# A two-layer attention kernel: attn1's row sums moved behind all of attn3's values, and four units in place of two between the last squares of layer 0 and their variance

## The chip, the cores and the metric

The kernel runs on one core of one Trainium2 chip. The metric is the device time of one launch in microseconds (us). A core has a matmul engine (TensorE; PE in the profile, PEld for its weight loads), VectorE (DVE), ScalarE (ACT), GpSimd (POOL) and SyncE (SP), which here only issues DMAs. Each engine works through its own queue in order; semaphores tie the queues together.

## What is computed

The input x is (2, 512, 64, 32): two batches, 512 channels, 2048 positions (tokens). All is float32. Cut to what matters here:

```python
# layer 0: softmax attention of 8 heads of 64, with position embeddings in q and k
o = softmax(q @ k.T / 8) @ v
x = o @ Wout + bout + x
# layer 1: Nystrom attention with 256 landmarks, then a linear feed-forward map
h = layernorm(x);  q, k, v = split(h @ Wqkv);  q = q / 8
qL, kL = mean over groups of 8 tokens of q, k                 # 256 landmarks
attn1 = softmax(q @ kL.T); attn2 = softmax(qL @ kL.T); attn3 = softmax(qL @ k.T)
out = attn1 @ (pinv(attn2) @ (attn3 @ v)) + depthwise_conv33(v)   # pinv: 6 iterations
x = x + out @ Wout + bout
x = x + layernorm(x) @ w_lora.T @ W.T
```

## The kernel before

**Tiles.** Channels lie on the 128 partitions, and heads are worked in pairs of two (2 x 64 = 128 rows). There are 2 batches x 4 pairs = 8 pairs. Tokens are cut into NTB = 4 blocks of TB = 512 or NST = 16 of 128. PSUM holds matmul results in banks of 128 x 512; helpers hand them out in rotation by tag: `bank` (two buffers up to the end of layer 0, four later), `product_bank` (two), `side_bank` (one each).

**Order.** PE, DVE, ACT and POOL keep the order in which the program text issues their instructions. Python generators yield after a small piece of work (a unit), and `advance(gens, n)` lets them make up to n units and returns how many it made; an exhausted generator is dropped from the list. So the order on every engine is fixed when the program is built. SP's DMAs are ordered by the scheduler.

**End of layer 0.** Layer 0 ends, for batch 1, with a loop over the four blocks t. For each, `out0` makes the output projection (four units), and `norm0_steps`, through `statistics` (L983), the layer norm in steps: channel sums on DVE (L986, L987), the mean as a matmul (L990), subtraction (L991, DVE), squares on ACT (L994, L997) and their adding on DVE (L1002, L1003), the variance as a matmul with a constant 1/C (L1006), square root on ACT (L1008, with a table load), then a reciprocal (L1023), two multiplications by it on POOL (L1025) and DVE (L1026), and a store of the normalised block (L1027, POOL's queue). Between these steps PE is given units of two lists: `more_out`, the output projection of the next block (empty for the last one), and `more`, layer 1's work for batch 0, from `others`. That yields key and query projections (L1245, four matmuls of 512 columns each, copied by ACT at L1248, reduced by DVE at L1250 and L1253) and, in their midst, for the pair before, `attend` (L1274: landmark scores, exponentials, and on DVE row sums, reciprocal and normalisation of X, L1297 to L1303, head by head) and `gram` for each head (L1305: matmuls of the normalised X at L1313 into two banks, 257 and 129 columns wide, copied by ACT at L1320; DVE's L1322 takes column sums from the copies).

**The loop over pairs in layer 1.** For each pair n in the order batch 1, then batch 0, `pinv` (L1531) runs five iterations for both heads. In each, `square` transposes one block (`flip`: PE at L1528, ACT's copy at L1529) and multiplies (L1538, tiles pa and pb), and DVE combines (L1551, `less`). After each iteration it calls `chunk(c)` (L1955), which does other pairs' work, so that PE is busy while DVE finishes:

- the pair before (`before`, while c < `n_ones`; n_ones is 4 for n up to 5, else 3): attn1 for token block c: scores (L1595), exponentials (L1600), an add of the two landmark halves on DVE (`attn1_add`, L1604), the product with the pinv's result (`attn1_values`, L1611, tile av), row sums (`attn1_sums`: `sums_of`, L779, four matmuls against a tile of ones, 32 columns of the array each; ACT's copy at L1619) and `attn1_inverse`: reciprocal on DVE (L1624), then eight DMAs on SP that spread it over the rows (`spread`, L790). In the next chunk `attn1_end` multiplies av by it on DVE (L1631) and adds it to the convolution's result on POOL (L1632).
- the pair behind (`after`, absent for the last pair): attn3 for key blocks 2c and 2c+1: scores (L1367), exponentials (L1376), adds on DVE (L1381), and `attn3_values` (L1388, eight records of 256 columns, 64 columns of the array each).

In `chunk` the units stand in this order: attn1 scores and add, attn3 scores and adds, attn1 values, attn3 values of 2c, attn1 sums, attn3 values of 2c+1, attn1 inverse. The next thing on PE is the flip of the next iteration.

Of the kernel before, what the change touches and what calls it, by code (L numbers as in the profile page):

```python
# [663 lines left out]
def fast_path(  # L664
# [89 lines left out]
    def block_of(pool, tag, name):  # L754
        return pool.tile([P, KC, TB], F32, tag=tag, name=name)
# [37 lines left out]
    def advance(gens, n=1):  # L793


        made, i = 0, 0
        while made < n and i < len(gens):
            got = next(gens[i], gens)
            if got is gens:
                gens.pop(i)  # L800
            elif got is GAP:
                i += 1
            else:
                made += 1
        return made

    def drain(gen):
        for _ in gen:
            pass
# [49 lines left out]
    class Heads0:  # L859
# [61 lines left out]
        def values(self):  # L921
            for t in range(NTB):
                values_of_tokens(self.v, t, self.xbs[t], lambda k: wv_sb[:, k, self.cols], self.name)
                yield
# [289 lines left out]
    class Pair:  # L1214
# [310 lines left out]
        def flip(self, X, name):  # L1525
# [3 lines left out]
            nc.scalar.copy(X[:, 1, :P], tp[:, :P])  # L1529

        def pinv(self, chunk, last):  # L1531


# [27 lines left out]
            for it in range(PINV_ITERS - 1):  # L1561
                for h in range(2):
                    pr = square(M[h], f"pa_{it}_{h}_{self.name}")
                    less_in_blocks(R[h], 3.5 * CUBE, M[h], pr)
                    less_in_blocks(M[h], 3.25 / rest, M[h], pr)
                for h in range(2):
                    pr = square(R[h], f"pb_{it}_{h}_{self.name}")
                    less_in_blocks(M[h], rest, M[h], pr)
                chunk(it)
# [134 lines left out]
    def finish1_units(b, os, early):  # L1704
        for t in range(NTB):
            if t == NTB - 1 and early:
                f = early.pop()
                yield from f.out_units()
                yield from f.norm_units()
                yield from f.map_units(lambda m, name: bank(name))  # L1710
                return
            xb = block_of(lpool, "xr", f"xb_g_{b}_{t}")
            f = Finish1(b, t, os, xb, lambda: block_of(lpool, "xn", f"xn_g_{b}_{t}"), True)
            yield from gap(3 if t else 2)
            yield from f.out_units()
            yield from f.norm_units()
            yield from f.map_units(lambda m, name: bank(name))
# [59 lines left out]
    def others(b, xhs, last, after=lambda t: None):  # L1777

        for hp in range(1, NPAIR):
            pair = pairs[b][hp]  # L1780
            pair.begin()
            units = pair.keys_and_queries(kvpool, "k", xhs, after if hp + 1 == NPAIR else lambda t: None)
            next(units)
            yield
            yield from beside(last.front(), units)
            yield from units
            last = pair
# [8 lines left out]
    more = [others(0, xhs, pairs[0][0], load_next)]  # L1796
    b = B - 1

    def as_block(tile):
        return tile.rearrange("p a b -> p (a b)").rearrange("p (k n) -> p k n", k=KC)  # L1800
# [7 lines left out]
    def norm0(t):  # L1808
        part = apool.tile([P, 2, TB], F32, tag="acc", name=f"part_f0_{t}")
        return norm0_steps(b, t, xbs_[t % 2], xns_[t % 2], part)  # L1810

    def out0(t):
        xb = xbs_[t % 2]
        nc.sync.dma_start(xb, chunked(x[b])[:, :, t * TB : (t + 1) * TB])
        return out0_units(b, t, xb, oTs)
# [4 lines left out]
    for t in range(NTB):  # L1820
        more_out = [out0(t + 1)] if t + 1 < NTB else []
        advance(more)

        next(norm)
        advance(more_out or more)
        if last is not None:
            next(last)
        advance(more_out or more)
        next(norm)
        advance(more_out, 2)  # L1830
        advance(more, 2)

        next(norm)
        last = norm
        while more_out:
            advance(more_out)
        if t + 1 < NTB:
            norm = norm0(t + 1)
            next(norm)
# [50 lines left out]
    def late_buffer(name):  # L1890

        return block_of(xpool, "xb", name).rearrange("p k n -> p (k n)")
# [37 lines left out]
    for n, pair in enumerate(todo):  # L1930
        before = todo[n - 1] if n else None
        after = todo[n + 1] if n + 1 < len(todo) else None
        if n + 2 < len(todo):
            todo[n + 2].prefetch_w()
        if n == NPAIR + 2:
            before.load_o(kvpool.tile([P, S], F32, tag="k", name=f"o2_{n - 1}"))
        if n == NPAIR + 3:

            xb = as_block(kvpool.tile([P, NST, P], F32, tag="v", name="xb_g_early"))
            xn = lambda: block_of(lpool, "xn", "xn_g_early")  # L1940
            early.append(Finish1(1, NTB - 1, [p.o for p in todo[:NPAIR]], xb, xn, True))
            before.load_o(late_buffer(f"o2_{n - 1}"))
        pair.iteration_start()
        while vals:
            advance(vals)
        if after:
            after.prefetch()
            after.attn3_begin()
        if n + 2 < len(todo):
            vals = [values(n + 2)]  # L1950
        if n:
            q = late_buffer if n > NPAIR + 1 else lambda name: kvpool.tile([P, S], F32, tag="k", name=name)
            pair.prefetch1(q(f"q2_{pair.name}"))

        def chunk(c):  # L1955
            nonlocal landmarks
            if before and 0 < c <= n_ones:
                before.attn1_end(c - 1)
            if n == NPAIR and c == 1:

                finish.append(finish1_units(1, [p.o for p in todo[:NPAIR]], early))
            advance(finish)
            if c == NTB:
                if after:
                    landmarks = after.landmarks_values()
                    next(landmarks)
                    drain(convolution(n + 1))
                else:
                    advance(finish, 2)
                return  # L1970
            ones_before = before if c < n_ones else None
            if ones_before:
                if c:
                    before.attn1_scores(c, 0)
                    before.attn1_scores(c, 1)
                before.attn1_add(c)
            if after:
                for s, bank_of in ((2 * c, product_bank), (2 * c + 1, bank)):
                    after.attn3_scores(s, bank_of)
                    after.attn3_add(s)  # L1980
            else:
                advance(finish)
            if ones_before:
                before.attn1_values(c)
            if after:
                after.attn3_values(2 * c)
            else:
                advance(finish)
            if ones_before:
                before.attn1_sums(c)  # L1990
            if after:
                after.attn3_values(2 * c + 1)
            if ones_before:
                before.attn1_inverse(c)
            if n == NPAIR + 2 and c % 2:
                advance(finish)

        def last(i):
            nonlocal start
            if i == 1 and after:  # L2000
                next(landmarks)
                drain(landmarks)
                start = after.start_values()
            if i == 2 and after:
                next(start)
            else:
                advance(vals)
            if i == 3 and after:
                next(start)
            if n_ones < NTB:  # L2010

                if i == 0:
                    before.attn1_scores(n_ones, 0)
                    before.attn1_scores(n_ones, 1)
                    before.attn1_add(n_ones)
                if i == 1:
                    before.attn1_values(n_ones)
                if i == 2:
                    before.attn1_sums(n_ones)
                if i == 3:  # L2020
                    before.attn1_inverse(n_ones)
                if i == 5:
                    before.attn1_end(n_ones)
            if i == 5:
                pair.attn1_scores(0, 0)
                pair.attn1_scores(0, 1)
            advance(finish)

        landmarks = start = None
        n_ones = NTB if n + 2 < len(todo) else NTB - 1  # L2030
        pair.pinv(chunk, last)

    def last_attn1():
# [156 lines left out]
```

## Time and profile before

| what | us |
|---|---|
| median of three runs (lowest, highest) | 2738.82 (2737.63, 2741.3) |
| the profiled execution's own time | 2739.02 |
| its span, first to last instruction | 2737.2 |
| PE busy in it | 2695.4 (98%) |
| DVE, ACT, POOL busy | 1631.7, 906.3, 162.0 |
| PE idle ahead of L1006 (variance), longest | 3.7 |
| PE idle ahead of L779 in attn1 (row sums, 128 matmuls) | 0.0 |

In the lines that follow, a timeline line has the start in us, the time it covers, the engine, the line of the kernel, the instruction, output<-inputs, the array's shape in use for matmuls (contraction rows\*columns), shapes, and how many were merged; in brackets the idle time ahead of it and what ended it. A float32 matmul appears as two records. A line of stretches has the length, then for PE, PEld, DVE, ACT and POOL the busy time (and instructions), then the granted clock of PE, the share of the DMA engines and GB/s. A busy PE in the profile is not PE at its peak: the ends of matmuls are modelled, so short stops between matmuls hide in busy time and are read from the starts.

### The profile page before, as it was taken

To read this page: it belongs to the slowest core of one execution; us is meant where nothing else is said; L and a number is where in the kernel's file an instruction comes from. 1 tells how busy PE (TensorE), PEld (TensorE's weight loads), DVE (VectorE), ACT (ScalarE), POOL (GpSimd) and SP (SyncE) were. 2 spreads that over 40 slices of the span, in tenths; PEclk is the share of its full clock that TensorE was granted. 3 is DMA by queue.
4 is the path that set the end of the run, shared out by engine and by line. 5 is a ranking of instruction groups with operands and counts; after the bars stand their busy time and mean duration, and the time that the engine had idled before them with its cause. 6 is when DMAs were issued, how large, how long until landed. Compare 5 with 4: busy or idle time off the path is not lost.

```text
span 2737.2 us, 41174 instructions
## 1 busy us (share of the span) xinstructions
PE 2695.4 (98%) x16994; PEld 1361.0 (50%) x16994; DVE 1631.7 (60%) x2087; ACT 906.3 (33%) x1352; POOL 162.0 (6%) x109
## 2 busy tenths in 40 slices
PE   9999999999999999999999999999999999999999
PEld 5343343434443334344344455777677666655344
DVE  3867777664557765656667544445544645465565
ACT  1434444434334334444422223223323223231210
POOL 0101011000001100000002000000000000000000
PEclk9999999999999999999999999999999999999999
DMA  4100000212111200012024632312211112111211
GB/s 147 41 11 24 24 24 24 86 36 70 32 63 57 97 24 20 24 40 77 24 89 163 209 120 93 103 34 87 81 37 62 59 44 87 44 60 53 89 39 47
DMA packets 111476, 173.99 MB, mean 64 GB/s; under 512 B 16176, under 2 KB 67888, under 8 KB 106672
## 3 DMA queue, kind: packets, MB, share of 16 engines
q1 hardware_dynamic: 105136, 150.00, 16.9%
q0 software_dynamic: 5440, 20.97, 2.1%
q8 instruction: 135, 2.21, 0.3%
q14 instruction: 61, 0.50, 0.1%
q10 hardware_dynamic: 704, 0.31, 0.0%
HBM read 90.87 MB, written 63.57 MB: 56 GB/s over the span
## 4 chain that ended last, share of the span: by engine, by line
PE 91%; DVE 5%; DMA 1%; ACT 1%; SPq 1%; issue 1%; POOL 0%; DVEq 0%; ACTq 0%; POOLq 0%
PE sc_f L1072 15%; PE av_f L1102 15%; PE pp L1245 8%; PE pa L1538 5%; PE pb L1538 5%; PE vp_f L953 4%; PE vp L953 4%; PE pp_k_f L905 4%; PE yp_g L968 4%; PE yp_f L968 4%; PE fp_g L1694 4%; PE pp_q_f L905 3%; PE av L1388 2%; PE sc L1367 2%; PE sc L1595 2%; PE av L1611 2%
## 5 line engine op out<-in xcount | busy, mean ns | idle before, releaser
L1090 DVE TENSOR_TENSOR acc_f<-acc_f,p_f 128x1024 f32<-128x1024 f32 x448 | 581.3, 1297 | 209.9 <-ACT p_f L1080 181.4
L1080 ACT ACTIVATE p_f<-sc_f 128x1024 f32<-128x1024 f32 x512 | 496.7, 1022 | 563.9 <-PE sc_f L1072 561.2
L1072 PE MATMUL sc_f<-q_f,k_f 64*64 64x512 f32 x4096 | 491.1, 594 | 2.7 <-ACT p_f L1080 2.7
L1102 PE MATMUL av_f<-p_f,v_f 64*64 64x512 f32 x4096 | 484.3, 589 | 0.0
L1102 PEld LDWEIGHTS av_f<-p_f,v_f 64*64 64x64 f32 x4096 | 156.5, 133 | 283.0 <-issue 283.0
L1072 PEld LDWEIGHTS sc_f<-q_f,k_f 64*64 64x64 f32 x4096 | 145.8, 133 | 285.6 <-issue 261.9
L1245 PE MATMUL pp<-xh,w 128*128 128x512 f32 x512 | 229.5, 600 | 0.7 <-ACT q L1248 0.7
L1538 PE MATMUL pa<-M 128*128 128x192 f32 (+1 forms) x640 | 153.1, 384 | 6.0 <-ACT M L1529 6.0
L1245 PEld LDWEIGHTS pp<-xh,w 128*128 128x128 f32 x512 | 95.3, 191 | 121.3 <-issue 113.8
L1538 PE MATMUL pb<-R 128*128 128x192 f32 (+1 forms) x640 | 149.3, 380 | 0.0
L1538 PEld LDWEIGHTS pa<-M 128*128 128x128 f32 x640 | 109.3, 195 | 27.6 <-ACT M L1529 9.1
L953 PEld LDWEIGHTS vp_f<-wv_f,x 128*128 128x128 f32 x1024 | 115.7, 192 | 13.5 <-issue 11.8
L953 PE MATMUL vp<-w,xh 128*128 128x128 f32 x1024 | 120.9, 276 | 0.0
L953 PEld LDWEIGHTS vp<-w,xh 128*128 128x128 f32 x1024 | 117.0, 192 | 7.2 <-issue 4.6
L905 PE MATMUL pp_k_f<-x,wk_f 128*128 128x512 f32 x256 | 116.0, 606 | 2.8 <-DVE k_f L908 2.4
L953 PE MATMUL vp_f<-wv_f,x 128*128 128x128 f32 x1024 | 118.7, 277 | 0.0
L1538 PEld LDWEIGHTS pb<-R 128*128 128x128 f32 x640 | 106.5, 190 | 23.2 <-DVE M L1551 0.4
L905 PE MATMUL pp_q_f<-x,wq_f 128*128 128x512 f32 x256 | 114.2, 598 | 0.8 <-DVE q_f L908 0.5
L968 PE MATMUL yp_g<-o,wo_f 128*128 128x512 f32 x256 | 114.8, 597 | 0.0
L968 PE MATMUL yp_f<-q_f,wo_f 128*128 128x512 f32 x256 | 113.5, 598 | 0.8 <-DVE xr_f L975 0.8
L1120 POOL TENSOR_TENSOR q_f<-q_f,rinv_f 128x512 f32<-128x512 f32 x32 | 46.7, 1459 | 1039.3 <-DMA rinv_f<-acc_f 761.1
L1551 DVE SCALAR_TENSOR_TENSOR R<-M,pa 128x320 f32<-128x320 f32 (+1 forms) x160 | 59.9, 416 | 67.8 <-PE pa L1538 67.8
(210 smaller groups left out, 2764.8 us busy)
## 6 DMA issues: line engine op xcount, KB each, us to landing
xh<-xh_fd SPq DMA_DIRECT2D x12, 1024.0 KB, 5.5
rinv_f<-acc_f SPq DMA_DIRECT2D x256, 32.0 KB, 1.9
xr_f<-in_x_dram SPq DMA_DIRECT2D x8, 1024.0 KB, 5.2
x_fd<-xr_f POOLq DMA_DIRECT2D x8, 1024.0 KB, 4.8
xh_fd<-xn_f POOLq DMA_DIRECT2D x8, 1024.0 KB, 4.7
k_fd<-k SPq DMA_DIRECT2D x32, 256.0 KB, 2.9
q_fd<-q SPq DMA_DIRECT2D x32, 256.0 KB, 2.9
k<-k_fd SPq DMA_DIRECT2D x8, 1024.0 KB, 6.6
```

Source lines behind the costliest of these rows:

```text
L905: nc.tensor.matmul(pp, lhsT=w_sb[kind][:, k, cols], rhs=xbs[t][:, k, :], start=k == 0, stop=k == KC - 1)
L953: nc.tensor.matmul(vp[:, j * P : (j + 1) * P], lhsT=xb[:, k, j * P : (j + 1) * P], rhs=w_of(k), start=k == 0, stop=k == KC - 1,)
L968: nc.tensor.matmul(yp, lhsT=wo_sb[:, k, m * P : (m + 1) * P], rhs=oTs[k][:, toks], start=k == 0, stop=k == NPAIR - 1,)
L1072: nc.tensor.matmul(sc[r * D : (r + 1) * D, h, :], lhsT=hd.k[rows, lo : lo + D], rhs=hd.q[rows, t * TB : (t + 1) * TB], start=True, stop=True,)
L1080: nc.scalar.activation(p, sc, AF.Exp, scale=D**-0.5)
L1090: nc.vector.tensor_tensor(acc, first if c == 1 else acc, p, ALU.add)
L1102: nc.tensor.matmul(av[r][half, :], lhsT=hd.v[keys, c, half], rhs=pp[keys, h, :], start=c == 0, stop=c == NST - 1,)
L1245: nc.tensor.matmul(pp, lhsT=self.w[j][:, c, :], rhs=xhs[t][:, c, :], start=c == 0, stop=c == KC - 1)
L1367: nc.tensor.matmul(scs[h][:, j * LM : (j + 1) * LM], lhsT=self.k[rows, c * P : (c + 1) * P], rhs=self.L[0][rows, :], start=True, stop=True,)
L1538: nc.tensor.matmul(dst, lhsT=lhsT[:, k, t * P : (t + 1) * P], rhs=rhs[:, k, :], start=k == 0, stop=k == 1)
L1551: nc.vector.scalar_tensor_tensor(out, m, scale, pr, ALU.mult, ALU.subtract)
L1694: nc.tensor.matmul(fp[:, cols], lhsT=mT[:, k, m * P : (m + 1) * P], rhs=self.xn[:, k, cols], start=k == 0, stop=k == KC - 1,)
```

## The change

Two edits, both to the order of issue. The first: where the loop at the end of layer 0 made up to two units of `more_out` and then two of `more`, it now makes four of `more` if `more_out` made none. `more_out` is empty only in the last pass. The second: in `chunk`, `attn1_sums` is issued behind the second `attn3_values` rather than between the two.

```diff
@@ the loop over t at the end of layer 0
         advance(more_out or more)
         next(norm)
-        advance(more_out, 2)
-        advance(more, 2)
+        advance(more, 2 if advance(more_out, 2) else 4)
 
         next(norm)
         last = norm
@@ chunk(c)
                 after.attn3_values(2 * c)
             else:
                 advance(finish)
-            if ones_before:
-                before.attn1_sums(c)
             if after:
                 after.attn3_values(2 * c + 1)
             if ones_before:
+                before.attn1_sums(c)
                 before.attn1_inverse(c)
```

The order of PE's instructions moves so, in the last pass of the first loop: before, query projection, variance, key projection, gram of head 0, gram of head 1; after, query projection, key projection, gram of head 0, variance, gram of head 1. On DVE the two copies L1322 pass the reciprocal L1023 and the multiplication L1026; on ACT the key's copy and the two copies of head 0's gram pass the table load and the square root.

## The prediction

> **What bounds the kernel now.** I read the page first, then the list of PE's waits, then the timelines around the two edits, then granted clock by stretch. On the page:
>
> ```profile
> PE 2695.4 (98%) x16994; PEld 1361.0 (50%) x16994; DVE 1631.7 (60%) x2087; ACT 906.3 (33%) x1352; POOL 162.0 (6%) x109
> PE 91%; DVE 5%; DMA 1%; ACT 1%; SPq 1%; issue 1%; POOL 0%; DVEq 0%; ACTq 0%; POOLq 0%
> ```
>
> PE is the bound and the chain runs along it, so an edit pays only what it takes out of PE's own stream: an idle gap, or time lost between matmuls. Neither edit removes a matmul. PE's waits (total us, times, longest):
>
> ```profile
> PE pa L1538 <- ACT M L1529: 6.0, 2, 4.6
> PE var_n L1006 <- issue: 3.7, 1, 3.7
> ```
>
> The second is the variance matmul of layer 0's last block, where the projection edit acts. In the stretch 1830 to 2440 us, where the sums edit acts, PE's five listed waits come to 5.0 us and none is at L779 or L1388. So the sums wait for nothing, and that edit can only gain between the matmuls.
>
> First place, PE, then the DVE work that it waits for:
>
> ```profile
> 1492.30 1.02 PE L1245 MATMUL pp<-xh,w 128*128 128x512 f32 x2
> 1497.00 1.48 PE L1006 MATMUL var_n<-xr_f,mean_w 128*128 128x512 f32 x2 [3.68 <-issue]
> 1498.28 4.95 PE L1245 MATMUL pp<-xh,w 128*128 128x512 f32 x8
> 1503.07 3.08 PE L1313 MATMUL pr<-X 128*128 128x257 f32 x16
> 1506.16 1.13 PE L1245 MATMUL pp<-xh,w 128*128 128x512 f32 x2
> ```
>
> ```profile
> 1492.20 1.58 DVE L1269 TENSOR_TENSOR bound<-most 128x1 f32<-128x1 f32 x1
> 1496.21 0.69 DVE L1003 TENSOR_TENSOR xr_f<-xr_f 128x512 f32<-128x512 f32 x1
> 1497.75 0.69 DVE L1299 TENSOR_TENSOR X<-X,rs 128x512 f32<-128x512 f32 x1
> 1499.99 0.69 DVE L1299 TENSOR_TENSOR X<-X,rs 128x512 f32<-128x512 f32 x1
> ```
>
> "Issue" names no releaser, but L1003, which makes the variance's input, ends at 1496.90 and PE starts 0.10 later: the wait is for DVE. The next two lines matter as much: the normalised X of each head, which gram (L1313) multiplies, is ready at 1498.44 and 1500.68. The projection behind the gap took 4.95 for what takes 3.43 elsewhere (eight records 0.429 apart). The stretches say why (PE busy, then granted clock):
>
> ```profile
> 1494.17:1497.58 3.41, 0.58 (x2) 0.37 (x3) 3.34 (x8) 0.00 (x0) 0.69 (x1) 1.00 0.76 282
> 1497.58:1500.99 3.41, 3.41 (x6) 1.35 (x5) 3.24 (x7) 1.97 (x2) 0.00 (x0) 0.50 0.50 181
> 2436.24:2439.65 3.41, 1.90 (x9) 0.56 (x8) 2.83 (x4) 0.78 (x3) 0.00 (x0) 1.00 0.53 154
> 2439.65:2443.07 3.42, 2.87 (x25) 1.70 (x26) 0.69 (x3) 0.84 (x3) 0.00 (x0) 1.00 0.00 0
> 2521.57:2524.98 3.41, 1.40 (x8) 0.89 (x6) 2.66 (x3) 0.00 (x0) 1.27 (x1) 1.00 0.04 10
> ```
>
> A 3.41 us stretch that is 83% idle is followed by half clock; one 59% idle (the last line) is too, in the records of granted clock; one 44% idle is not.
>
> Second place, one chunk of today's order, and one of the last pair, which already has the order that the change makes (sums straight ahead of the flip, L1528):
>
> ```profile
> 1838.06 1.03 PE L1388 MATMUL av<-p,v 128*64 128x256 f32 x8
> 1839.02 0.64 PE L779 MATMUL rs<-acc,ones 128*32 128x256 f32 x8
> 1839.59 1.08 PE L1388 MATMUL av<-p,v 128*64 128x256 f32 x8
> 1840.60 0.33 PE L1528 MATMUL p_pa<-ident,M 128*128 128x128 f32 x1
> ```
>
> ```profile
> 2474.57 0.64 PE L779 MATMUL rs<-acc,ones 128*32 128x256 f32 x8
> 2475.14 0.33 PE L1528 MATMUL p_pa<-ident,M 128*128 128x128 f32 x1
> ```
>
> Note the array forms: 128\*64, 128\*32, 128\*64, 128\*128.
>
> [...] within a form these records start 0.216 apart, over each of the three changes 0.31. [...] the 128x1 L1269 lasts 1.58 and ends with POOL's L1025 (1490.45 to 1493.77), its seven fellows average about 0.15. [...] the trace has 1.28 ahead of the square root.
>
> **Part 1, the projections.** The condition differs only in the last pass: earlier, two output units are made and two units follow as before. In the last, four units follow. By the PE order of both kernels these are attend, a query projection, and new ahead of the variance a key projection (4 matmuls) and gram of head 0; so "four projections" is one projection and one gram more. DVE's order is the same through both L1299. So:
> - The key projection starts at 1493.15 (last record 1492.72 plus 0.43) and issues 3.43: to 1496.6. Its bank is free (the copy ended at 1489.3).
> - Gram 0 needs X at 1498.44, plus 0.10: 1498.54. PE still waits, about 1.8 between records.
> - Gram 0 issues 4 x 0.216 and 4 x about 0.13. The ordinary banks are two in rotation, so the variance takes the one that the 257-wide copy (L1320) frees: last record 1499.24, copy 0.41 later, 0.38 long, variance at 1500.08.
> - Variance: two records, with a slow first step about 0.93. Gram 1 (X at 1500.68, no wait) begins at 1501.0; its first half issues to 1501.9.
> - Its second half takes the variance's bank. ACT must end first: table load at 1501.24, 1.28, square root 0.69: 1503.2. A new wait of 1.2.
> - Second half 0.5 and start-up 0.1: next projection at 1503.9, against 1506.16 now. **Gain 2.3.**
>
> The half clock goes (of the present loss about 1.7), since the new gaps, 1.8 and 1.2, fill at most about 37% of a window on today's phase. Were a window to hold all of the first gap it would be 53% idle, between 44 and 59, unknown: half clock then costs 1.7. Bounds of this part: +0.6 and +3.5 (no bank wait); I take 2.3. Moved besides: on ACT the copies of gram 0 pass the table load (its end was worked in); on DVE two csum copies pass the 3.34 reciprocal, which may start at about 1504.3 against 1505.08; on SP the second X store passes behind k_fd and two A stores, 0.3 to 0.6 each, read only many us later. POOL's multiply and the xh store come no later than now. Work after 1506 waits on PE, not on an absolute time, so the gain is kept.
>
> **Part 2, the sums.** In the stretch 1830 to 2440 the copy L1619 occurs 23 times: five pairs with four chunks, one with three. That is where the edit moves anything; the last pair has no values to pass.
> - Now: 1838.06 to 1840.60 is 2.54.
> - After: first values group 4 x 0.216 = 0.86, the second to the sums 0.96 (as from 1838.06 to 1839.02), sums to flip 0.57 (2474.57 to 2475.14): 2.39.
> - Difference 0.15, one change of form and the slow first step after it. 23 x 0.15 = **3.5**.
>
> Does anything make PE wait? The second values start 0.67 earlier and need ACT's exponentials, which end 1.74 before that start in a first chunk, 1.09 in most, 0.80 in the worst. The copy L1619 now comes 0.86 later, just ahead of the flip's copy L1529, and the reciprocal (1.75 on DVE) 1.0 later as PE's work stands: L1551's first subtraction waits about 0.1. In the last pair that order stands already: reciprocal 2475.69 to 2477.44, subtraction at 2477.36, and flip to the first pb matmul 3.84, the same as now in the others. So zero on PE. Behind the reciprocal SP's eight spread DMAs start later, and DVE's L1631 of the next chunk, which waits for them: today 1848.94, just as they land, so 0.9 later by PE's work; POOL's multiply then locks L1604 out for about 0.5. DVE is idle 1.73 ahead of L1604, and PE's next av1 matmul is 2.1 behind L1631's end: covered. Without that cover it costs up to 0.5 a chunk. Bounds: 0.15 lost to 0.2 gained a chunk, -3.5 to +4.6; I take 3.5, for the last pair shows it.
>
> **Sum.** 2.3 + 3.5 = 5.8, from the profiled 2739.02 (span 2737.20 and 1.8 around it) to 2733.3. The median of the runs, 2738.82, is 0.2 lower: 2733.1, or -0.21%. A measurement tells about 0.2%, 5.5 us, from no change; the forecast lies at its edge.
>
> **Rivals.**
> - *The wait only moves (0.20).* Gram 0's wait for X and the square root's bank are joined by a half-clock window: part 1 gives 0.6, 2734.7. For it: the 53% above[...]. Against: 44% idle left the clock whole.
> - *The change of form isn't saved (0.10).* [...] part 2 gives 0: 2736.5. Against: the last pair's 0.57.
> - *The late sums stall the pinv step (0.06).* Sums' copy, flip's copy and reciprocal come in series at the chunk's end; if PE's pa matmul waits the copy's 0.37 in each of 23 chunks, 8.5 lost against 5.8 and 2741.5, slower. It decides from 0.25 a chunk. Against: L1529 ends 0.4 before its weight load at 1841.69 and is delayed by 0.1 or less; for it: PE did wait for this copy elsewhere.
> - *No bank wait (0.04).* 2731.9.
>
> Forecast 0.60. Its own spread with the measurement, about 0.8, puts 0.6 of it beyond -0.2%. With the last rival, and a little of the first: faster 0.43, same 0.51, slower 0.06. The range, 2731.5 to 2736.0, takes in the first rival and the upper bound and leaves out most of the second and all of the third.
>
> **What would show it.** Right: L1006's last start near 1500 with a gap near 1.8 ahead of L1313 and one near 1.2 inside it, full clock there; the projection after at 1503.9; 1838.06 to flip 2.39 in all 23 chunks; no new PE wait at L1538. Wrong: half clock again near 1500; L1529 or L1551 as PE's releaser from 1830 to 2440; a step from sums to flip over 0.57.

## The result and the profile after

| | before | after |
|---|---|---|
| median of 13 runs (lowest, highest), us | 2738.54 (2734.91, 2741.74) | 2732.43 (2731.32, 2735.85) |
| profiled execution's own time | 2739.02 | 2732.18 |
| its span | 2737.2 | 2730.4 |

The ratio of the times is 0.998, with a 95% interval of 0.9973 to 0.9988. The medians differ by 6.1 us where 5.8 were forecast.

First the page of after, busy time and the chain that ended last:

```profile
PE 2688.2 (98%) x16994; PEld 1361.7 (50%) x16994; DVE 1628.1 (60%) x2087; ACT 903.7 (33%) x1352; POOL 161.8 (6%) x109
...
PE 90%; DVE 5%; DMA 1%; SPq 1%; ACT 1%; issue 1%; POOL 0%; DVEq 0%; ACTq 0%; POOLq 0%
```

Nothing has changed in kind: the same 16994 matmul records on PE, and PE is the bound. The list of PE's waits (total us, times, longest) has lost the variance's 3.7 and has three new lines where the two edits act. Two of them:

```profile
PE pr L1313 <- DVE X L1299: 1.8, 1, 1.8
...
PE pr L1313 <- ACT rstd_n L1008: 1.2, 1, 1.2
```

The third, 0.5 ahead of the pb matmul (L1538), is shown below. To see where time was gained, I took the start of every PE record in both profiled executions and subtracted. The shift, after minus before, changes in a few places only:

| stretch (us of before) | change of the shift | what lies there |
|---|---|---|
| 0 to 1490 | -2.45 | nearly all between 11 and 37: the first loads, and a window of half clock in before, none in after; not the edit |
| 1490 to 1515 | -2.31 | the last variance of layer 0: part 1 |
| 1836 to 2411 | -3.47 | the 23 chunks: part 2 |
| 2411 to 2430 | +0.46 | the last of these chunks |
| 2430 to 2470 | -0.31 | also in the projections alone, -0.35 |
| 2470 to 2526 | +0.27 | also in the projections alone, +0.27 |
| 2526 to 2600 | +0.8 | DMAs of a spread that land about 0.9 late |

So the 6.8 us between these two spans aren't all the edit's. The first line is layer 0's first block waiting for x, and it differs from execution to execution: at 1490 the nine other profiled executions are 0.7 to 3.0 us ahead of this one of before. Near 34 us before has one window of half clock, as have two of the other nine (the projections alone and the sums alone, the two that are only 0.7 ahead); after has none. Of the kernels below only the sums alone have the last line too (0.65).

Part 1, PE in after:

```profile
1488.12 6.17 PE L1245 MATMUL pp<-xh,w 128*128 128x512 f32 x14
1496.14 1.55 PE L1313 MATMUL pr<-X 128*128 128x257 f32 x8 [1.85 <-DVE X L1299]
1497.71 1.12 PE L1006 MATMUL var_n<-xr_f,mean_w 128*128 128x512 f32 x2
1498.68 1.03 PE L1313 MATMUL pr<-X 128*128 128x257 f32 x4
1500.94 0.71 PE L1313 MATMUL pr<-X 128*128 128x129 f32 x4 [1.24 <-ACT rstd_n L1008]
1501.49 5.74 PE L1245 MATMUL pp<-xh,w 128*128 128x512 f32 x13
```

The 3.68 ahead of L1006 has become two waits, 1.85 for the X of head 0 and 1.24 for the bank that the square root must empty first. The projection behind starts at 1501.49; with the 2.45 of the start put back that is 1503.94. ACT shows the second wait from the other side:

```profile
1498.91 1.28 ACT L1008 ACT_TABLE_LOAD   x1 [0.91 <-PE var_n L1006]
1500.20 0.69 ACT L1008 ACTIVATE rstd_n<-var_n,eps 128x512 f32<-128x512 f32 x1
1500.79 0.37 ACT L1320 COPY A<-pr 128x257 f32<-128x257 f32 x1
```

The square root ends at 1500.89 and PE goes on 0.05 later. In the stretches (length, then PE busy; granted clock is the first bare number behind the engines) there is no half clock:

```profile
1493.36:1496.77 3.41, 1.56 (x6) 0.71 (x5) 3.27 (x9) 0.59 (x1) 0.00 (x0) 1.00 0.81 304
1496.77:1500.18 3.41, 2.92 (x13) 1.73 (x11) 3.31 (x7) 1.91 (x3) 0.00 (x0) 1.00 0.73 249
```

The whole first gap fell into one window, 54% idle, and the window after it was granted full clock.

Part 2, one chunk of after on PE:

```profile
1833.30 1.90 PE L1388 MATMUL av<-p,v 128*64 128x256 f32 x16
1835.12 0.64 PE L779 MATMUL rs<-acc,ones 128*32 128x256 f32 x8
1835.69 0.33 PE L1528 MATMUL p_pa<-ident,M 128*128 128x128 f32 x1
```

From 1833.30 to 1835.69 is 2.39, in place of 2.54. The same stretch is 0.15 shorter than in before in each of the 23 chunks.

### The profile page after: what moved, and what is told of

It reads as the page before. It is cut to its first block, busy times and chain, and to the rows that moved or that the text cites. A ratio compares the mean times of both kernels' runs of the same rounds, so it can differ in the third digit from the quotient of the medians.

```text
span 2730.4 us, 41173 instructions
## 1 busy us (share of the span) xinstructions
PE 2688.2 (98%) x16994; PEld 1361.7 (50%) x16994; DVE 1628.1 (60%) x2087; ACT 903.7 (33%) x1352; POOL 161.8 (6%) x109
## 4 chain that ended last, share of the span: by engine, by line
PE 90%; DVE 5%; DMA 1%; SPq 1%; ACT 1%; issue 1%; POOL 0%; DVEq 0%; ACTq 0%; POOLq 0%
PE sc_f L1072 15%; PE av_f L1102 15%; PE pp L1245 8%; PE pb L1538 5%; PE pa L1538 5%; PE vp_f L953 4%; PE vp L953 4%; PE pp_k_f L905 4%; PE yp_g L968 4%; PE yp_f L968 4%; PE fp_g L1694 3%; PE pp_q_f L905 3%; PE sc L1367 2%; PE sc L1595 2%; PE av L1611 2%; PE av L1388 2%
## 5 line engine op out<-in xcount | busy, mean ns | idle before, releaser
L1538 PE MATMUL pa<-M 128*128 128x192 f32 (+1 forms) x640 | 153.2, 385 | 6.3 <-ACT M L1529 6.3
L1538 PE MATMUL pb<-R 128*128 128x192 f32 (+1 forms) x640 | 149.3, 380 | 0.5 <-DVE M L1551 0.5
L1538 PEld LDWEIGHTS pa<-M 128*128 128x128 f32 x640 | 109.3, 195 | 27.8 <-ACT M L1529 9.4
L1538 PEld LDWEIGHTS pb<-R 128*128 128x128 f32 x640 | 106.5, 190 | 23.6 <-DVE M L1551 0.8
L1694 PE MATMUL fp_g<-xn_g,mT 128*128 128x512 f32 (+1 forms) x232 | 99.8, 580 | 0.0
```

The lines of the kernel that those rows point to most:

```text
L1538: nc.tensor.matmul(dst, lhsT=lhsT[:, k, t * P : (t + 1) * P], rhs=rhs[:, k, :], start=k == 0, stop=k == 1)
L1694: nc.tensor.matmul(fp[:, cols], lhsT=mT[:, k, m * P : (m + 1) * P], rhs=self.xn[:, k, cols], start=k == 0, stop=k == KC - 1,)
```

## The experiments

The theory: part 1 moves the wait and shortens it, with the half clock behind it gone; part 2 saves one change of array form in each chunk and makes nobody wait. The rivals: only the half clock counts in part 1; the place of the sums counts in part 2, not the number of changes. Shifts are counted as in the table above, against the profiled execution of before.

**Each part alone.** Two kernels, each with one hunk of the change.

> The projection edit alone. Theory (part 1 is a wait of its own, worth 2.3): 2736.3 against 2738.5 of before, ratio 0.9992; the projection behind gram 1 starts 2.3 earlier than before once the start-up's offset is taken out, no half clock near 1500, and the shift does not change between 1506 and 2400. Rival (the two parts are not independent, or the half clock comes back): gain under 1.

> The sums edit alone. Theory (one change of array form saved per chunk, 0.15 x 23): 2735.1, ratio 0.9987; the stretch from the first values group to the flip falls from 2.54 to 2.39 in each of 23 chunks, and one place, the pair with three chunks, gives back about 0.5 because DVE's L1631 lands late. Rival (the gain came from part 1 alone, or from the start-up's offset): ratio 1.000 and 2.54 unchanged.

The projections alone: 2736.18 against 2738.11, ratio 0.9992 (0.9986 to 0.9999). The shift changes by -2.31 at 1490 to 1515 and not at all from 1515 to 2411. The sums alone: 2734.22, ratio 0.9986 (0.9979 to 0.9992); -3.47 from 1836 to 2411. The parts add up: the two shifts in the profile are those of the whole change, to 0.01. In this execution of the second kernel the old gap stood, and cost more than in before:

```profile
1495.08:1498.49 3.41, 2.16 (x3) 1.16 (x4) 3.27 (x9) 0.03 (x1) 0.00 (x0) 0.50 0.82 309
1498.49:1501.90 3.41, 3.41 (x5) 1.34 (x5) 3.31 (x7) 1.94 (x2) 0.00 (x0) 0.50 0.42 144
```

Here 6.8 us of half clock go with the same 3.7 us gap that was followed by 3.4 in before, and the variance itself falls into it. The shift grows by 1.08 up to 1515 for that.

**The sums elsewhere.** If the number of changes of array form counts, sums ahead of both groups of values save nothing, since there the order is 64, 32, 64, 128 columns again. The edit is shown against the change; the first loop of this kernel is before's.

```diff
             if ones_before:
                 before.attn1_values(c)
+                if after:
+                    before.attn1_sums(c)
             if after:
                 after.attn3_values(2 * c)
 ...
             if ones_before:
-                before.attn1_sums(c)
+                if not after:
+                    before.attn1_sums(c)
                 before.attn1_inverse(c)
```

> As the change, but the sums stand ahead of both values groups, right behind attn1's values. Theory (only the number of changes of array form counts): as many changes as in before, so the chunk takes 2.54 again, part 2 gives nothing, 2736.3, ratio 0.9992. Rival (what counts is that the two values groups are together, or that the sums are late): 2.39, ratio 0.998. Rival 2 (sums wait for their operand when they come early): over 2.54 and slower than before.

The number in this expectation is wrong: it counts part 1, which this kernel doesn't have, and what the theory gives for it is before's own time, a ratio of 1.000. Measured: 2737.47, ratio 0.9997 (0.9989 to 1.0005), and the shift from 1836 to 2411 changes by 0.00. PE in this kernel:

```profile
1833.42 1.94 PE L1611 MATMUL av<-p,u 128*64 128x512 f32 x8
1835.29 0.64 PE L779 MATMUL rs<-acc,ones 128*32 128x256 f32 x8
1835.86 1.95 PE L1388 MATMUL av<-p,v 128*64 128x256 f32 x16
1837.73 0.33 PE L1528 MATMUL p_pa<-ident,M 128*128 128x128 f32 x1
```

From L1611, itself 64 columns wide, the forms go 64, 32, 64, 128: three changes, as in before; in the change it is two (64, 32, 128). The order is another, the changes are the same, and so is the time. What counts is the changes of form in the order, not where the sums stand.

**What is the half clock worth?** Before's order, with the gap filled: four matmuls of 512 columns that nothing reads stand ahead of the last variance, so that PE is busy in the gap and the wait itself is not shortened.

```diff
         advance(more, 2)
+        if t + 1 == NTB:
+            fill = scores_bank("fill")
+            for i in range(4):
+                nc.tensor.matmul(fill[:, i % 2, :], lhsT=mean_w, rhs=xhs[1][:, i, :], start=True, stop=True)
```

> Before's order, with four matmuls of 512 columns added ahead of the last block's variance, into a bank that nothing reads; the outputs are the reference's. They fill the 3.7 gap and remove no wait of DVE. Theory (the gap costs 3.7 by itself and about 1.7 more by the half clock behind it): no half clock near 1500, the variance starts where it did, the next query projection starts about 1.7 earlier than in before; 2736.6, ratio 0.9994. Rival (only the idle time counts): no shift, ratio 1.000.

```profile
1490.19 3.70 PE L1836 MATMUL fill<-xh,mean_w 128*128 128x512 f32 x8
1494.00 1.12 PE L1006 MATMUL var_n<-xr_f,mean_w 128*128 128x512 f32 x2
1494.96 3.60 PE L1245 MATMUL pp<-xh,w 128*128 128x512 f32 x8
```

```profile
1493.30:1496.70 3.40, 3.29 (x9) 1.27 (x8) 3.30 (x8) 1.48 (x2) 0.00 (x0) 1.00 0.68 255
1496.70:1500.10 3.40, 3.40 (x14) 2.04 (x13) 3.30 (x7) 1.57 (x4) 0.00 (x0) 1.00 0.47 160
```

The granted clock is 1.00 in both stretches. The projection takes 3.60 over eight records in place of 4.95, and the shift at 1490 to 1515 changes by -1.71, as expected. So useless work in a gap is worth 1.7 us here, and of part 1's 2.31, 0.6 is the shorter wait. Timed, this kernel gains more: 2734.48 against 2738.67, ratio 0.9986 (0.998 to 0.9993), at least 1.9 us by the interval. The gap of before can cost two windows of half clock, as in the sums-only kernel, but that hardly fills the difference: the granted clocks listed with the runs average 0.9974 for before and 0.9981 here, from which I estimate that the clock cost about 2 us less over the whole kernel ((1 - clock) x time). What the rest of the timed gain is stays open.

**Three units instead of four.** With gram 0 left behind the variance, the variance needn't wait for X.

```diff
-        advance(more, 2 if advance(more_out, 2) else 4)
+        advance(more, 2 if advance(more_out, 2) else 3)
```

> Three units in the last pass instead of four, so that gram of head 0 stays behind the variance. Theory (gram's wait for the normalised X and for the square root's bank are what is left of the gap): the variance starts at about 1497.0 in the clock of before with a gap of 0.3, gram 0 waits 0.5 for X, its second half 0.5 for the bank, the next query projection starts at 1502.3 against 1503.9 with four: 1.6 faster than the change, 2730.8, ratio 0.9972. Rival (four units are the right cover): equal to the change or slower, 2732.4.

```profile
1494.71 1.10 PE L1006 MATMUL var_n<-xr_f,mean_w 128*128 128x512 f32 x2 [0.26 <-issue]
1496.30 1.11 PE L1313 MATMUL pr<-X 128*128 128x257 f32 x4 [0.49 <-DVE X L1299]
1497.92 2.17 PE L1313 MATMUL pr<-X 128*128 128x129 f32 x12 [0.52 <-ACT rstd_n L1008]
1500.11 7.13 PE L1245 MATMUL pp<-xh,w 128*128 128x512 f32 x16
```

The three gaps come to 1.27, where the change has 3.09. The shift at 1490 to 1515 is -3.75, so 1.44 better than the change. The times, 2731.87 and 0.9977 (0.997 to 0.9984), can't tell it from the change: the profile shows it, the timing doesn't.

**A bank of its own for the variance.** The change, and the last variance takes half of a scores bank, so that gram 1 needn't wait for the square root.

```diff
-        var = bank(f"var_{name}")
+        var = (var_bank or bank)(f"var_{name}")
 ...
+        apart_bank = lambda name: scores_bank(name)[:, 0, :]
+        var_bank = apart_bank if b and t == NTB - 1 else None
```

> The change, with the last block's variance in a score bank instead of the two ordinary ones. Theory (gram 1's second half waits 1.24 only for the bank that the square root frees): that wait is gone, the wait of 1.85 for X stays, the projection behind starts 1.2 to 1.4 earlier than with the change; 2731.2, ratio 0.9973. Rival (ACT's table load and square root are in the way themselves, since gram's copies queue behind them): the wait only moves to the next bank, gain under 0.4.

My theory fell. The lines of this kernel stand 2 lower, so L1315 is the gram:

```profile
1498.33 1.54 PE L1315 MATMUL pr<-X 128*128 128x257 f32 x8
1500.86 6.70 PE L1247 MATMUL pp<-xh,w 128*128 128x512 f32 x15 [0.99 <-ACT A L1322]
```

Gram 1 now runs through, and the projection behind it waits 0.99 for a copy. On ACT the copies of gram 1 still stand behind the table load and the square root (1.28 us from 1498.56, then 0.69; the copies start at 1500.44), and the projection takes the next bank that they empty. At 1515 it is 0.47 better than the change, not the 1.2 of the wait and near the rival's "under 0.4". The bank was where the wait was seen; its source is ACT's queue. The whole: 2731.76, ratio 0.9975 (0.9964 to 0.9986).

**The one exposed chunk.** In after, the last of the 23 chunks gives 0.46 back. DVE, POOL and PE there:

```profile
2406.87 0.69 DVE L1631 TENSOR_TENSOR rinv<-av,rinv 128x512 f32<-128x512 f32 x1 [1.73 <-DMA rinv<-acc]
2407.48 3.42 DVE L1381 TENSOR_TENSOR acc<-acc,p 128x1024 f32<-128x1024 f32 x2
2407.64 2.18 POOL L1632 TENSOR_TENSOR o<-o,rinv 128x512 f32<-128x512 f32 x1 [14.96 <-DVE rinv L1631]
...
2410.83 2.27 DVE L991 TENSOR_TENSOR xn_g<-xb_g,mean_g 128x2048 f32<-128x2048 f32 x1
...
2414.48 1.99 PE L1538 MATMUL pb<-R 128*128 128x192 f32 x8 [0.50 <-DVE M L1551]
```

The same place in before:

```profile
2414.23 0.69 DVE L1631 TENSOR_TENSOR rinv<-av,rinv 128x512 f32<-128x512 f32 x1 [0.85 <-DMA rinv<-acc]
...
2415.30 3.37 DVE L1381 TENSOR_TENSOR acc<-acc,p 128x1024 f32<-128x1024 f32 x2 [0.38 <-ACT p L1376]
```

L1631 waited 0.85 for the spread reciprocals, not 1.73. Two things are special here. The pair has attn1 in only three of its chunks and this is the fourth, so no L1604 follows L1631, and DVE's idle time behind L1631 is 0.38, where a usual chunk of before has 1.73. And the 2.27 us subtraction L991 of the layer norm stands ahead of the pinv's combine with no idle time. So of 0.88 later at L1631, 0.38 is covered and PE's pb matmul waits the other 0.50. The next kernel puts back the early place of the sums in the one chunk ahead of it.

```diff
+            early_sums = ones_before and after and n_ones < NTB and c == 2
+            if early_sums:
+                before.attn1_sums(c)
             if after:
                 after.attn3_values(2 * c + 1)
             if ones_before:
-                before.attn1_sums(c)
+                if not early_sums:
+                    before.attn1_sums(c)
```

> The change, but in one chunk of the 23, the last of the pair with three chunks, the sums stay between the two values groups. Theory (there the late sums make L1631 wait for its spread DMAs, and DVE's subtractions for PE's pb come late, 0.50): PE's wait for DVE M at pb is gone, L1631 waits about 0.85 rather than 1.73, the shift against before changes by under 0.1 between 2411 and 2430 rather than by +0.46, and 0.15 is not gained in that chunk. Rival (that wait has nothing to do with the sums): still about 0.5.

PE's wait is gone, and the give-back falls from 0.46 to 0.09 for 0.15 lost in the chunk itself; one run of it took 2731.09. But L1631 still waits 1.35, not the 0.85 expected:

```profile
2406.78 0.69 DVE L1631 TENSOR_TENSOR rinv<-av,rinv 128x512 f32<-128x512 f32 x1 [1.35 <-DMA rinv<-acc]
```

So the landings of the eight DMAs vary by themselves. Over all ten profiled executions this chunk reads so: with the sums early (five kernels, before among them) L1631 waits 0.81 to 1.35 and PE nothing; with the sums late (five) it waits 1.32 to 1.93, and PE waits 0.46 to 0.60 in four of them and nothing in the sums-only kernel, the one with 1.32. So in these ten PE waits when L1631 has waited 1.69 or more, and not at 1.35 or less. The late sums bring it there in four executions of five, the early ones in none; when the DMAs land decides the rest. That the lateness reaches PE through DVE is shown by the lines above.

**The largest wait, which the change left alone.** PE's 4.9 us at L1538 come in the last pair: ACT has the three squares of the layer norm (L994, L997) ahead of the flip's copy L1529, and they wait for L991. In after:

```profile
PE pa L1538 <- ACT M L1529: 6.3, 2, 4.9
```

```profile
2517.45 1.06 ACT L994 ACTIVATE sq_g<-xn_g 128x1024 f32<-128x1024 f32 x1 [6.11 <-DVE xn_g L991]
2518.41 1.13 ACT L997 ACTIVATE sq_g<-xn_g 128x512 f32<-128x512 f32 x2
2519.45 0.24 ACT L1529 COPY M<-p_pa 128x128 f32<-128x128 f32 x1
```

In the next kernel, with three units as above, that step is taken one chunk later.

```diff
             if c == NTB:
 ...
                 else:
+                    advance(finish)
                     advance(finish, 2)
 ...
             if after:
                 after.attn3_values(2 * c)
-            else:
+            elif c < NTB - 1:
                 advance(finish)
```

> Three units as before this call, and besides, in the last pair's fourth chunk the squares of the layer norm are issued one chunk later, so that ACT's copy for the flip doesn't stand behind them. Theory (the largest wait left on PE, 4.6 to 5.1 for ACT M at pa near 2520, is that queue, and it brings 6.8 of half clock): the wait falls to about 1.3, now for DVE behind the subtraction L991, no or one stretch of half clock; about 7 faster than three units alone, 2725, ratio 0.995. Rival (DVE's subtraction holds PE for as long): gain under 2.

```profile
PE pa L1538 <- ACT M L1529: 1.4, 1, 1.4
PE pb L1538 <- DVE M L1551: 1.2, 2, 0.6
```

The 4.9 us wait is gone (1.4 elsewhere is left), and so are the 6.8 us of half clock behind it (granted clock 1.00 from 2511 to 2523). The shift from 2470 to 2535 is -5.57, against +0.49 in the kernel with three units alone: 6.1 gained, for 7 expected; new waits of 0.3 and 0.6 at the step's new neighbours account for most of the rest. Timed 2726.16 against 2738.67, ratio 0.996 (0.9946 to 0.9973): the fastest kernel of these.

## Why the prediction was right

- **Part 1, gain 2.3: measured 2.31**, in the change and alone. The steps hold one by one: gap ahead of gram 0 "about 1.8" (1.85), "a new wait of 1.2" for the variance's bank (1.24), "next projection at 1503.9" (1503.94 with the start's shift put back). Filling the gap gave 1.71 for "about 1.7" of half clock.
- **The half clock goes.** The reason given, that the gaps fill at most about 37% of a window, did not hold: in all four kernels with the change's order in this place (after, projections alone, one early, own bank) the whole first gap fell into one window, 54% idle. That was the case the prediction had called unknown, and the clock stayed whole. So this part came out right by luck, as far as was known then. The first rival didn't happen; its price was right, for without the half clock's 1.71 part 1 would be worth 0.6.
- **Part 2, 0.15 in each of 23 chunks: measured 3.47** for 3.5. The last pair's lines gave the size, 0.57 from the sums to the flip; in after the same step takes 0.57 too (1835.12 to 1835.69). Sums placed with as many changes as in before gained 0.00. The second rival falls.
- **"Zero on PE" for the late sums** held in 22 chunks. The third rival is not seen: no PE wait for L1529 between 1830 and 2440 but one of 1.4 that stood there already.
- **The step that failed: L1631 0.9 later is "covered".** In the last chunk L1631 waited 0.88 longer, and PE 0.50. The cover was worked out for a usual chunk, with DVE's 1.73 of idle time ahead of L1604. That L1604 runs longer when it starts while POOL is in its 1.27 us L1632, for which the prediction put 0.5, is seen five times in after: it takes 1.36 to 2.14 there, against a median of 1.22. This chunk has no L1604, only 0.38 of idle time, and a 2.27 us step of the layer norm ahead of the combine. The price, "up to 0.5 a chunk" without that cover, was right; that one chunk of 23 lacks most of it wasn't seen.
- **The sum.** In the places where the edits act the profile shows 2.31 + 3.47 - 0.46 = 5.3, for 5.8 forecast. The medians say 6.1, with an interval of 3.3 to 7.4. That the forecast lies within 0.3 of the medians shows little at this size; the places in the profile are the sharper instrument, since the start alone moves by over 2 us between executions.

## What to carry to other kernels

A wait that is moved is worth its new length, worked out step by step, plus the half clock that it no longer triggers; here the clock was three quarters of part 1's gain. Where TensorE is the bound, group matmuls of one array form: each saved change was worth 0.15 us here. And when work is put later in a loop, look for the one iteration that differs from the usual one, by a step that it lacks or one that it has besides, for that is where the cover ends.

## What the runs showed of the hardware

Half clock also follows windows that are only partly idle. In before its stretches start at 33.26, 1497.58, 2524.99 and 2733.21 us, which are 429, 301 and 61 times 3.413 us apart. So I cut each execution into windows of 3.41 us on the grid of its own clock records. For the windows that decide:

| kernel | window, us | granted clock in it | PE busy in it | granted clock in the next |
|---|---|---|---|---|
| before | 1494.17 to 1497.58 | 1.00 | 0.58 | 0.50 |
| after | 2513.94 to 2517.35 | 1.00 | 0.93 | 0.50 |
| before | 29.85 to 33.26 | 1.00 | 1.01 | 0.50 |
| gap filled | 2433.35 to 2436.76 | 1.00 | 1.35 | 0.50 |
| own bank | 2428.88 to 2432.29 | 1.00 | 1.35 | 0.50 |
| sums alone | 30.77 to 34.18 | 1.00 | 1.38 | 0.50 |
| before | 2521.57 to 2524.98 | 1.00 | 1.40 | 0.50 |
| sums alone | 2433.74 to 2437.15 | 1.00 | 1.42 | 1.00 |
| after | 1493.36 to 1496.77 | 1.00 | 1.56 | 1.00 |
| squares later | 2429.35 to 2432.77 | 1.00 | 1.57 | 1.00 |
| after | 2428.60 to 2432.02 | 1.00 | 1.76 | 1.00 |
| before | 2436.24 to 2439.65 | 1.00 | 1.90 | 1.00 |
| before | 2524.98 to 2528.40 | 0.50 | 0.84 | 0.50 |
| after | 2517.35 to 2520.76 | 0.50 | 1.01 | 0.50 |
| sums alone | 1495.08 to 1498.49 | 0.50 | 2.16 | 0.50 |
| before | 1497.58 to 1500.99 | 0.50 | 3.41 | 1.00 |
| after | 2520.76 to 2524.17 | 0.50 | 3.41 | 1.00 |

At full clock, a window with PE busy for 1.40 us or less (59% idle or more) was followed by half clock, one with 1.42 or more was not. No other window of before or of after, from 3 us on, is at odds with that; of all ten profiled executions one is, in a start-up: busy for 1.53 and half clock behind it. The edge is read from these traces afterwards, and PE's busy time is modelled in part. To get out of half clock took more: with 2.16 us busy another window of half clock followed, with 3.41 full clock. That is how the gap of the sums-only kernel came to cost 6.8 us of half clock: the first of its two windows was busy for 2.16.

So the same gap of 2.1 us (PE's wait ahead of L1513) near 2435 us costs nothing or, in the own-bank kernel, 1.7 (its shift grows by 1.69 from 2430 to 2470), by where it falls on the grid. Two kernels there, sums alone and own bank:

```profile
2433.74:2437.15 3.41, 1.42 (x8) 0.36 (x4) 3.31 (x6) 0.30 (x2) 0.00 (x0) 1.00 0.52 144
2437.15:2440.57 3.42, 3.35 (x26) 1.92 (x27) 0.21 (x2) 1.31 (x4) 0.00 (x0) 1.00 0.00 0
```

```profile
2428.88:2432.29 3.41, 1.35 (x9) 0.45 (x7) 3.10 (x6) 0.00 (x0) 0.00 (x0) 1.00 0.38 116
2432.29:2435.70 3.41, 3.41 (x20) 1.75 (x19) 0.00 (x0) 0.43 (x2) 0.00 (x0) 0.50 0.00 0
```

A busy time of 1.42 kept full clock, 1.35 did not. So an edit that moves the whole program can win or lose such a window far from its own place, and it is likely one reason why runs of one kernel differ by several microseconds: of 62 runs of before, the thirty that list a mean clock of 0.997 average 2738.9 us, the seven with 0.999 average 2736.1.
